# Sums in the order of x, zero borders written in the prologue, the residual inside silu's products, and the last strips' statistics taken one by one

## The chip, the cores and the metric

The kernel runs on one core of a Trainium2 chip. The metric is the device time of one execution, in microseconds (us). The core has five engines that take instructions in their own order and wait for each other by semaphores: TensorE (PE, matrix products), VectorE (DVE), ScalarE (ACT), GpSimd (POOL) and SyncE (SP, which here only issues DMAs). POOL and ACT can issue DMAs too. The fast memory has 128 partitions; a tile written "128x512" has 512 floats in each.

## The reference

Two layers on x of shape 4 x 16 x 256 x 256 (batch, channel, row, column), everything in fp32. `_gn` is a group norm with 8 groups of 2 channels.

```python
def _L0_conv_ref(x, conv_w, conv_b):
    out = jax.lax.conv_general_dilated(x, conv_w, window_strides=(1, 1), padding='SAME', ...) + conv_b[None, :, None, None]
    logits = out.reshape(N, C, K * K, H, W)          # C = 16, K = 5: 400 logits a pixel
    weights = jax.nn.softmax(logits, axis=2)
    return jnp.einsum('ncuij,ncuij->ncij', _unfold(x), weights)   # 5x5 patches, weighted

def _L1_conv_ref(x, base_weight, spline_weight, spline_scaler, bias_weight):
    patches = _extract_patches(x, KSIZE, STRIDE, PAD)             # 3x3
    bspl = _b_splines(patches, grid)                              # 8 cubic bases of each value
    out = jnp.einsum('bjhwn,ijn->bihw', jax.nn.silu(patches), base_w)
    out = out + jnp.einsum('bjhwns,ijns->bihw', bspl, spl_w)
    return out + bias_weight[None, :, None, None]

x = x + _L0_conv_ref(_gn(x), L0_conv_conv_w, L0_conv_conv_b)
x = x + _L1_conv_ref(_gn(x), L1_conv_base_weight, ...)
```

So layer 0 makes, for every pixel and channel, 25 logits by a 3x3 convolution, and averages the 5x5 patch by their softmax. Layer 1 is a convolution of silu(x) and of eight spline bases of x.

## The kernel before

**Prologue.** It loads x, takes batch statistics, prepares the weights, and normalizes batch 0 into three scratch areas in DRAM: `hs` (patches), `hst` and `hsl` (the convolution's operands, high and low parts). `normalize(b, ...)` is a generator: each `next` does one piece. Its first piece writes the zero borders of these areas by twelve DMAs (lines 256, 262 and 263); for batch 0 they go on POOL's queue, for the batches 1 to 3 on SP's. Batch b+1 is normalized while layer 0 works on batch b, one piece per step; its x loads are line 276, the tile is `xp`, and ACT's normalizing lines are 323 and 336. `prepare0` and `prepare1` prepare the weights of the two layers; a part of both runs on POOL.

**Layer 0.** There are 64 strips (4 batches, 2 halves of 128 rows, 8 strips of 32 columns), with the row in the partition. A strip has 8 steps of 4 columns. A step does, each on its own engine:

- PE: the logits `lg` (lines 791 and 795), into PSUM
- ACT: their exponentials into `e[:, 0]` (line 814)
- POOL: `e[:, 1] = e[:, 0] * u`, the product with the patches (line 819)
- DVE: one reduction over the 25 taps of both halves of `e`, into `nd` (line 691). This is done two steps late.

After a strip's last reduction, with delays counted in steps (`after(k, f)` puts f k steps later): ACT takes the reciprocal of the denominator as Ln and Exp (`seed`, lines 704 and 705), DVE refines it and multiplies (`divide`, lines 709, 710 and 713), POOL subtracts the result from x in place (`apply`, line 719; the sign is turned in line 710). `nd` holds columns then channels, x holds channels then columns, so line 713 writes `o` transposed:

```python
o = ndp.tile([P, C, SW], F32, name=f"o_{n}{arm}", tag="o", bufs=2)
nc.vector.tensor_mul(o.rearrange("p c j -> p j c"), nd[:, 1], r)
```

The x tile `xc` holds four strips (CX = 128 columns). When its last strip is subtracted, `statistics` runs once for each of 8 groups on ACT (line 731: Identity, then Square, each with an accumulated sum; the written values go to the scratch tile `z` and are not used), and `store` writes the tile to `x1s` in DRAM (line 740, ACT's queue). `e` has four buffers, `nd` and `xc` three each, `z` two in the pool `l0`.

**Layer 1.** There are 64 units of 16 rows. The splines need, for a row of the unit, the distance of each value to the bases' centres: SP loads replicated rows into `xta`, `xtb`, `xtc` in turn, ACT takes the absolute distance (line 942) and squares (lines 164, 166 and 167), DVE does the rest (lines 159, 168, 169 and 170), in two halves of the unit with the temporaries `ta` and `tb`; line 170 writes `ring`, from which PE reads. `silu` (ACT, line 924) reads the tile `sx` (64 partitions: 4 rows of 16 channels) and writes `sl`. The output `yp` of a unit is 128 products: 96 of `ring` with `wt` (line 988), 8 of `sx` with an identity `wx`, which is the residual x (line 996), and 24 of `sl` with `ws` (line 1004). DVE adds the bias into `yo` (line 971) and SP stores it.

**Order.** `in_order` fixes every engine's instructions in the order in which they were written. Layer 1's first instructions may start ahead of layer 0's end on two engines only, behind marks that layer 0 leaves (`marks[SPE]`, `marks[ACTE]`); the first silu comes behind layer 0's last ACT instruction. Layer 1's tiles take the memory of layer 0's pools when these are free.

Of the kernel before, what the change touches and what calls it, by code (L numbers as in the profile page):

```python
# [11 lines left out]
F32 = mybir.dt.float32  # L12
# [4 lines left out]
PSUM = bass.MemoryType.PSUM  # L17
DRAM = bass.MemoryType.DRAM


# [13 lines left out]
def conv_preact_kernel(  # L34
# [84 lines left out]
    nc.gpsimd.memset(wt, 0.0)  # L119
    ws = const.tile([RD * C, 3, RT, C], F32, name="ws")  # L120
    nc.gpsimd.memset(ws, 0.0)

    wx = const.tile([RD * C, RT, C], F32, name="wx")
    nc.gpsimd.memset(wx, 0.0)
    for r in range(RT):
        p = SROWS.index(r + 1) * C
        nc.sync.dma_start(wx[p : p + C, r], ident[p : p + C, p : p + C])

# [4 lines left out]
    NK = NH * W // CX  # L133
    st1 = [const.tile([P, 2, G, NK], F32, name=f"st1_{b}") for b in range(B)]

# [111 lines left out]

    def normalize(b, ptr, tiles, held=None, copier=None, queue=nc.sync):

# [3 lines left out]
        copier = copier or nc.scalar.copy  # L253
        for e in (0, HP - PAD):
            for r in range(PAD):
                queue.dma_start(
                    hs[b][:, e + r].rearrange("s c w -> c s w"),
                    zero[0:C, 0 : NST * SP].rearrange("c (s w) -> c s w", s=NST),
                )
        for h in range(NH):  # L260
            for w in (0, (W + 1) * RP):
                queue.dma_start(hst[b][h][:, w : w + RP], zero[0:C, 0:RP])
                queue.dma_start(
                    hsl[b][h][:, :, w : w + RP].rearrange("c t r -> (c t) r"), zero[:, 0:RP]
                )

        moves = []
# [132 lines left out]
    with tc.tile_pool(name="prep0", bufs=2) as prep, tc.tile_pool(  # L400
# [121 lines left out]
        for b in range(B):  # L522
# [38 lines left out]
            nc.vector.tensor_scalar(v, v, 9.0 / 8.0, ms[:, 0:1], ALU.mult, ALU.add)  # L561
            nc.vector.tensor_scalar(v, v, ms[:, 1:2], None, ALU.mult)
            if b == 0:
                prepare0()
            if b == 1:
                prepare1()
            if b == 0:
                ahead = normalize(0, ptr0, tiles, held, nc.vector.tensor_copy, nc.gpsimd)
                next(ahead)
# [41 lines left out]
    def layer0(shift):  # L611
# [4 lines left out]
        with tc.tile_pool(name=f"prep{arm}", bufs=2) as prep, tc.tile_pool(  # L616
# [62 lines left out]
            def after(k, f, *args):  # L679

                later.append([k, partial(f, *args)])
# [7 lines left out]
            def sums():  # L689
                nd, j, e, done = waiting.pop(0)  # L690
                nc.vector.tensor_reduce(  # L691
                    nd[:, :, j : j + JG, :], e.rearrange("p t j m c d -> p t j c m d"),
                    AX.XY, ALU.add,
                )
                if done is not None:
                    done()
# [5 lines left out]
            def seed(n, nd, xc):  # L702
                r = prc.tile([P, SW, C], F32, name=f"r_{n}{arm}", tag="r")
                nc.scalar.activation(r, nd[:, 0], AF.Ln)
                nc.scalar.activation(r, r, AF.Exp, scale=-1.0)
                after(1, divide, n, nd, xc, r)

            def divide(n, nd, xc, r):
                nc.vector.tensor_mul(nd[:, 0], nd[:, 0], r)
                nc.vector.scalar_tensor_tensor(r, nd[:, 0], 2.0, r, ALU.subtract, ALU.mult)  # L710

                o = ndp.tile([P, C, SW], F32, name=f"o_{n}{arm}", tag="o", bufs=2)
                nc.vector.tensor_mul(o.rearrange("p c j -> p j c"), nd[:, 1], r)  # L713
                after(LAG + 3, apply, n, o, xc)

            def apply(n, o, xc):
                w0 = strips[n][2] * SW % CX
                v = xc[:, :, w0 : w0 + SW]
                nc.gpsimd.tensor_sub(v, v, o)  # L719
                if w0 + SW == CX:  # L720
                    for g in range(G):
                        after(1 + g, statistics, n, xc, g)
                    after(2, store, n, xc)

            def statistics(n, xc, g):
                b, hf, s = strips[n]
                k = hf * (W // CX) + s * SW // CX
                z = l0.tile([P, GC * CX], F32, name=f"z_{n}_{g}{arm}", tag="z")
                v = xc[:, g * GC : (g + 1) * GC, :].rearrange("p c w -> p (c w)")
                for t, f in enumerate((AF.Identity, AF.Square)):  # L730
                    nc.scalar.activation(  # L731
                        z, v, f, scale=nrm[b][:, 0, g : g + 1], bias=nrm[b][:, 1, g : g + 1],
                        accum_out=st1[b][:, t, g, k : k + 1],
                    )
# [21 lines left out]
            for n, (b, hf, s) in enumerate(strips):  # L756
# [14 lines left out]

                nd = ndp.tile([P, 2, SW, C], F32, name=f"nd_{n}{arm}", tag="nd")
                for j in range(0, SW, JG):
# [68 lines left out]
    def layer1(arm, last, marks):  # L842
# [3 lines left out]
        with ExitStack() as pools:  # L846
# [14 lines left out]
            xt0, tmp0 = fixed("xta", XT), temps("ta")  # L861
            sxp, yop = pool("sx", 2), pool("yo", 3)
            tmp1, xt1 = temps("tb"), fixed("xtb", XT)
            ring = fixed("ring", [P, 3 * RU + 2, W + 2])[0]
            sl, xtt = fixed("sl", [RD * C, RU // RT, W + 2], 2), xt0 + xt1 + fixed("xtc", XT)
            pad = fixed("pad", [P, W + 2])[0]
# [32 lines left out]


            def load_tiles(n):
                b, u = units[n]
                t = sxp.tile([RD * C, RU // RT, W], F32, name=f"sx_{n}{arm}", tag="sx")
                for p, q in outside(u):
                    nc.gpsimd.memset(t[p : p + C, q], 0.0)  # L905
                for k, d in enumerate(SROWS):
                    q0 = 1 if (u, d) == (0, 0) else 0
                    q1 = RU // RT - (1 if (u, d) == (NU - 1, RD - 1) else 0)
                    nc.sync.dma_start(
                        t[k * C : (k + 1) * C, q0:q1, :],  # L910
                        rows(x1s[b], [[CP, C], [RT * W, q1 - q0], [1, W]], u * RU - 1 + d + q0 * RT),
                    )
                return t

# [6 lines left out]

            def silu(n, t):
                b, u = units[n]
                nc.scalar.activation(  # L924
                    sl[n % 2][:, :, 1 : W + 1], t, AF.Silu,
                    scale=sc[b][0][0 : RD * C], bias=sc[b][1][0 : RD * C],
                )
                for p, q in outside(u):
                    nc.gpsimd.memset(sl[n % 2][p : p + C, q, 1 : W + 1], 0.0)

# [50 lines left out]

            def outputs(n, sx):
                b, u = units[n]
                yp = py.tile([P, 2, W], F32, name=f"yp_{n}{arm}", tag="yp")
                M, r0 = RT * C, place(n)
                for k, (d, e) in enumerate((d, e) for d in range(RD) for e in range(3)):
                    for t in range(NT):
                        nc.tensor.matmul(  # L988
                            yp[t * M : (t + 1) * M],
                            lhsT=wt[:, d, e].rearrange("p r o -> p (r o)"),  # L990
                            rhs=ring[:, r0 + t * RT + d : r0 + t * RT + d + 9 : 8, e : e + W],
                            start=k == 0, stop=False,
                        )

                for t in range(NT):
                    nc.tensor.matmul(  # L996
                        yp[t * M : (t + 1) * M],
                        lhsT=wx.rearrange("p r o -> p (r o)"),
                        rhs=sx[:, t : t + NT + 1 : NT],
                        start=False, stop=False,  # L1000
                    )
                for e in range(3):
                    for t in range(NT):
                        nc.tensor.matmul(  # L1004
                            yp[t * M : (t + 1) * M],
                            lhsT=ws[:, e].rearrange("p r o -> p (r o)"),
                            rhs=sl[n % 2][:, t : t + NT + 1 : NT, e : e + W],
                            start=False, stop=e == 2,
                        )
                waiting.append((b, u, yp))  # L1010
# [5 lines left out]
            for half in range(2):  # L1016
                load_x(0, half)
            sx = [load_tiles(0)]
            for half in range(2):
# [11 lines left out]
            first_silu = len(nc.cur_bb.bb.instructions)  # L1031
            silu(0, sx[0])
            for n in range(len(units)):
                if n % 2:
                    next(more, None)
                if n > 0:
                    features(n, put)
                    silu(n, sx[n])
                halo(n)
# [4 lines left out]
                if n + 1 < len(units):  # L1044
                    sx.append(load_tiles(n + 1))
                outputs(n, sx[n])
            for _ in range(LAG1):
# [59 lines left out]
```

## Time and profile before

| | us |
|---|---|
| median of three runs | 3093.68 (3092.81 to 3095.0) |
| the profiled execution | 3092.67 |
| its span, first to last instruction | 3090.9 |
| prologue, to the first strip | 0 to 119 |
| layer 0 | 119 to 2073 |
| layer 1 | 2073 to 3091 |

The largest groups, with their mean durations in ns:

| instruction | engine | how many | mean |
|---|---|---|---|
| reduction, line 691 | DVE | 512 | 3476 |
| products of `divide`, lines 709, 710, 713 | DVE | 64 each | 681, 696, 1083 |
| product with the patches, line 819 | POOL | 512 | 3547 |
| subtraction, line 719 | POOL | 64 | 1328 |
| exponentials, line 814 | ACT | 1024 | 837 |
| one pass of the statistics, line 731, and the read of its sum | ACT | 256 each | 600 and 192 |
| residual product, line 996 | PE | 512 | 601 |

How it is read: "busy" is the time in which an engine runs an instruction, and a bracket behind an instruction, such as `[11.10 <-POOL e L819]`, says how long its engine stood idle before it and which instruction ended that. Instructions of one engine overlap a little at their ends, so what one of them costs is read from start to start.

### The profile page before, as it was taken

Reading aid. Unit: us, or ns where it says so; the run is one execution under the profiler, and the core shown is the slowest. Engines: PE = TensorE matmul, PEld = TensorE weight load, DVE = VectorE, ACT = ScalarE, POOL = GpSimd, SP = SyncE. Lnnn points to the kernel's source line nnn. Section 1 sums busy time; section 2 is a strip of 40 time slices with the busy share of each in tenths; the row PEclk is TensorE's granted clock in tenths of the full one; section 3 lists DMA queues with packets and bytes.
Section 4 is the critical chain, followed back from the end, with each engine's and each line's share of the span. In section 5 each row is a group of like instructions: output and inputs, shape, how many; then the busy total and the mean of one; then the engine's idle time right before and its main releaser. Section 6 shows DMA issues by size and latency. Waiting matters only on the chain.

```text
span 3090.9 us, 40797 instructions
## 1 busy us (share of the span) xinstructions
PE 2840.5 (92%) x14760; PEld 1484.6 (48%) x14760; DVE 2976.4 (96%) x1571; ACT 2240.5 (72%) x2619; POOL 1951.1 (63%) x734
## 2 busy tenths in 40 slices
PE   4499999989999999999999999957999999999998
PEld 3366656656556666666666566632222222222222
DVE  7499999999999999999999999988999999999997
ACT  6466665676766566756646546559999999999995
POOL 4199999999999999999999999970100100000000
PEclk7699999999999999999999999988999999999999
DMA  9988977879878778878867667649999988999994
GB/s 275 284 222 224 249 203 206 219 189 255 230 206 240 191 202 224 242 214 218 221 161 199 164 171 193 156 110 201 194 193 197 197 194 191 197 196 198 193 198 89
DMA packets 352725, 626.36 MB, mean 203 GB/s; under 512 B 41330, under 2 KB 218724, under 8 KB 336644
## 3 DMA queue, kind: packets, MB, share of 16 engines
q1 hardware_dynamic: 318020, 605.29, 79.0%
q10 hardware_dynamic: 33024, 16.78, 1.9%
q8 instruction: 121, 1.98, 0.3%
q0 software_dynamic: 1472, 1.59, 0.2%
q14 instruction: 88, 0.72, 0.1%
HBM read 513.95 MB, written 104.24 MB: 200 GB/s over the span
## 4 chain that ended last, share of the span: by engine, by line
DVE 65%; PE 9%; ACT 9%; issue 8%; DMA 6%; SPq 2%; POOL 1%; DVEq 0%; ACTq 0%; POOLq 0%
DVE nd L691 45%; PE yp L988 3%; PE lg L791 3%; DVE ta L169 3%; DVE ta L168 3%; DVE tb L169 3%; DVE tb L168 3%; DMA sx<-x1s 2%; DVE ring L170 2%; DVE o L713 1%; DVE tb L159 1%; DVE r L710 1%; DMA an<-hsl 1%; ACT sl L924 1%; ACT ta L167 1%
## 5 line engine op out<-in xcount | busy, mean ns | idle before, releaser
L791 PE MATMUL lg<-wm,am 128*128 128x400 f32 x4096 | 1741.2, 506 | 102.9 <-ACT e L814 64.2
L819 POOL TENSOR_TENSOR e<-e,u 128x1600 f32<-128x1600 f32 x512 | 1789.9, 3547 | 67.7 <-ACT e L814 48.6
L691 DVE TENSOR_REDUCE nd<-e 128x128 f32<-128x3200 f32 x512 | 1746.9, 3476 | 31.6 <-POOL e L819 31.5
L795 PE MATMUL lg<-wn,an 97*128 97x400 f32 x2048 | 1349.7, 659 | 12.1 <-DMA an<-hsl 11.9
L814 ACT ACTIVATE e<-lg 128x800 f32<-128x800 f32 x1024 | 817.8, 837 | 726.4 <-DVE nd L691 522.3
L791 PEld LDWEIGHTS lg<-wm,am 128*128 128x128 f32 x4096 | 764.3, 193 | 424.1 <-ACT e L814 113.3
L988 PE MATMUL yp<-ring,wt 128*32 128x512 f32 x6144 | 739.7, 595 | 66.8 <-POOL ring L959 46.5
L795 PEld LDWEIGHTS lg<-wn,an 97*128 97x128 f32 x2048 | 389.3, 190 | 330.3 <-issue 21.1
L988 PEld LDWEIGHTS yp<-ring,wt 128*32 128x32 f32 x6144 | 206.9, 109 | 591.5 <-issue 470.0
L905 POOL MEMSET sx<- 16x256 f32 x8 | 2.4, 302 | 667.2 <-PE yp L996 232.5
L1004 PE MATMUL yp<-sl,ws 64*32 64x512 f32 x1536 | 176.5, 588 | 0.0
L731 ACT ACTIVATE z<-xc,nrm 128x256 f32<-128x256 f32 x256 | 153.6, 600 | 10.5 <-POOL xc L719 6.2
L170 DVE SCALAR_TENSOR_TENSOR ring<-ta,ta 128x2048 f32<-128x2048 f32 (+1 forms) x64 | 147.8, 2309 | 10.8 <-ACT z L731 8.3
L169 DVE TENSOR_TENSOR ta<-ta,ta 128x2048 f32<-128x2048 f32 (+1 forms) x64 | 148.4, 2318 | 2.9 <-ACT ta L167 2.9
L170 DVE SCALAR_TENSOR_TENSOR ring<-tb,tb 128x2048 f32<-128x2048 f32 x64 | 145.6, 2276 | 2.6
L169 DVE TENSOR_TENSOR tb<-tb,tb 128x2048 f32<-128x2048 f32 x64 | 145.2, 2268 | 0.7 <-ACT tb L167 0.7
L924 ACT ACTIVATE sl<-sx,q 64x2048 f32<-64x2048 f32 x64 | 133.4, 2085 | 1.5 <-DMA sx<-x1s 1.4
L194 POOL TENSOR_TENSOR d<-d,nrz 128x8 f32<-128x8 f32 x4 | 2.7, 663 | 200.1 <-DVE d L192 200.1
L167 ACT ACTIVATE ta<-ta 128x2048 f32<-128x2048 f32 (+1 forms) x64 | 123.2, 1925 | 2.0
L167 ACT ACTIVATE tb<-tb 128x2048 f32<-128x2048 f32 x64 | 120.5, 1883 | 0.0
L1004 PEld LDWEIGHTS yp<-sl,ws 64*32 64x32 f32 x1536 | 48.8, 106 | 116.2 <-issue 115.9
L719 POOL TENSOR_TENSOR xc<-xc,o 128x512 f32<-128x512 f32 x64 | 85.0, 1328 | 13.4 <-DVE o L713 13.4
(181 smaller groups left out, 2054.3 us busy)
## 6 DMA issues: line engine op xcount, KB each, us to landing
am<-hst SPq DMA_DIRECT2D x512, 194.6 KB
u<-hs SPq DMA_DIRECT2D x320, 288.0 KB
an<-hsl SPq DMA_DIRECT2D x512, 129.8 KB
xta<-x1s SPq DMA_DIRECT2D x40, 1024.0 KB
xtb<-x1s SPq DMA_DIRECT2D x40, 1024.0 KB
xtc<-x1s SPq DMA_DIRECT2D x40, 1024.0 KB
am<-hst SPq DMA_DIRECT2D x256, 129.8 KB
sx<-x1s SPq DMA_DIRECT2D x248, 128.0 KB
```

The lines of the kernel that those rows point to most:

```text
L167: nc.scalar.activation(s1, r1, AF.Square, scale=2.0)
L168: nc.vector.scalar_tensor_tensor(s2, t, 2.0, s2, ALU.subtract, ALU.mult)
L169: nc.vector.tensor_mul(s1, s1, r1)
L170: nc.vector.scalar_tensor_tensor(f, s2, 0.0, s1, ALU.min, ALU.subtract if given else ALU.add)
L691: nc.vector.tensor_reduce(nd[:, :, j : j + JG, :], e.rearrange("p t j m c d -> p t j c m d"), AX.XY, ALU.add,)
L791: nc.tensor.matmul(lg[:, i, :NL], lhsT=am[:, o : o + P], rhs=wm.rearrange("p m c d -> p (m c d)"), start=True, stop=False,)
L795: nc.tensor.matmul(lg[:, i, :NL], lhsT=an[:, o : o + P], rhs=wn.rearrange("p m c d -> p (m c d)"), start=False, stop=True,)
L814: nc.scalar.activation(ev, lg[:, :, :NL], AF.Exp)
L819: nc.gpsimd.tensor_tensor(e[:, 1].rearrange("p j m c d -> p j (m c) d"), e[:, 0].rearrange("p j m c d -> p j (m c) d"), uv, ALU.mult,)
L924: nc.scalar.activation(sl[n % 2][:, :, 1 : W + 1], t, AF.Silu, scale=sc[b][0][0 : RD * C], bias=sc[b][1][0 : RD * C],)
L988: nc.tensor.matmul(yp[t * M : (t + 1) * M], lhsT=wt[:, d, e].rearrange("p r o -> p (r o)"), rhs=ring[:, r0 + t * RT + d : r0 + t * RT + d ...
L1004: nc.tensor.matmul(yp[t * M : (t + 1) * M], lhsT=ws[:, e].rearrange("p r o -> p (r o)"), rhs=sl[n % 2][:, t : t + NT + 1 : NT, e : e + W], ...
```

## The change

Five edits go together.

1. *Zero borders.* A function `zeros(b)` issues the twelve DMAs of batch b on POOL's queue, and the prologue calls it for every batch, right after the batch's statistics. `normalize` no longer does so.
2. *Sums in the order of x.* `nd` is laid out as channels then columns. The reduction writes it in that order, its reads are unchanged; line 713 becomes an in-place product on `nd[:, 1]`; the tile `o` is gone, and the subtraction reads `nd[:, 1]`.
3. *Statistics of the last columns.* For the last four strips, `statistics` is called after each strip's subtraction on its 32 columns instead of once for 128; the table of sums of the last batch has three more columns.
4. *Scratch.* `z` moves from the pool `l0` (two buffers) to the pool `x1` of the x tiles (one buffer).
5. *Residual in silu's products.* SP loads the rows straight into partitions 64 to 127 of `sl`, which now has three buffers; silu reads these and writes partitions 0 to 63. The identity moves into the lower rows of the centre tap of `ws`, so that the eight centre products take 128 rows instead of 64, and the eight products with `wx` are gone: 120 products a unit. The tiles `sx` and `wx` are gone.

```diff
-    def normalize(b, ptr, tiles, held=None, copier=None, queue=nc.sync):
+    def zeros(b):
         for e in (0, HP - PAD):
             for r in range(PAD):
-                queue.dma_start(
+                nc.gpsimd.dma_start(
                     hs[b][:, e + r].rearrange("s c w -> c s w"),
...
+            zeros(b)
             if b == 0:
                 prepare0()
             if b == 1:
                 prepare1()
...
                 nc.vector.tensor_reduce(
-                    nd[:, :, j : j + JG, :], e.rearrange("p t j m c d -> p t j c m d"),
+                    nd[:, :, :, j : j + JG].rearrange("p t c j -> p t j c"),
+                    e.rearrange("p t j m c d -> p t j c m d"),
                     AX.XY, ALU.add,
                 )
...
                 nc.vector.scalar_tensor_tensor(r, nd[:, 0], 2.0, r, ALU.subtract, ALU.mult)
-
-                o = ndp.tile([P, C, SW], F32, name=f"o_{n}{arm}", tag="o", bufs=2)
-                nc.vector.tensor_mul(o.rearrange("p c j -> p j c"), nd[:, 1], r)
-                after(LAG + 3, apply, n, o, xc)
+                nc.vector.tensor_mul(nd[:, 1], nd[:, 1], r)
+                after(LAG + 3, apply, n, nd, xc)
...
-                nc.gpsimd.tensor_sub(v, v, o)
+                nc.gpsimd.tensor_sub(v, v, nd[:, 1])
+                few = n >= len(strips) - CX // SW
+                if few or w0 + SW == CX:
+                    for g in range(G):
+                        after(1 + g, statistics, n, xc, g, w0 if few else 0, w0 + SW)
                 if w0 + SW == CX:
-                    for g in range(G):
-                        after(1 + g, statistics, n, xc, g)
                     after(2, store, n, xc)
...
-                z = l0.tile([P, GC * CX], F32, name=f"z_{n}_{g}{arm}", tag="z")
+                z = x1p.tile([P, GC, CX], F32, name=f"z_{n}_{g}{arm}", tag="z", bufs=1)
...
-                nd = ndp.tile([P, 2, SW, C], F32, name=f"nd_{n}{arm}", tag="nd")
+                nd = ndp.tile([P, 2, C, SW], F32, name=f"nd_{n}{arm}", tag="nd")
...
-                t = sxp.tile([RD * C, RU // RT, W], F32, name=f"sx_{n}{arm}", tag="sx")
+                t = sl[n % 3][P // 2 :, :, 1 : W + 1]
...
+                t = sl[n % 3][0 : P // 2, :, 1 : W + 1]
                 nc.scalar.activation(
-                    sl[n % 2][:, :, 1 : W + 1], t, AF.Silu,
-                    scale=sc[b][0][0 : RD * C], bias=sc[b][1][0 : RD * C],
+                    t, sl[n % 3][P // 2 :, :, 1 : W + 1], AF.Silu,
+                    scale=sc[b][0][P // 2 :], bias=sc[b][1][P // 2 :],
                 )
...
-                for t in range(NT):
-                    nc.tensor.matmul(
-                        yp[t * M : (t + 1) * M],
-                        lhsT=wx.rearrange("p r o -> p (r o)"),
-                        rhs=sx[:, t : t + NT + 1 : NT],
-                        start=False, stop=False,
-                    )
                 for e in range(3):
                     for t in range(NT):
+                        v = slice(0, P if e == 1 else P // 2)
                         nc.tensor.matmul(
                             yp[t * M : (t + 1) * M],
-                            lhsT=ws[:, e].rearrange("p r o -> p (r o)"),
-                            rhs=sl[n % 2][:, t : t + NT + 1 : NT, e : e + W],
+                            lhsT=ws[v, e].rearrange("p r o -> p (r o)"),
+                            rhs=sl[n % 3][v, t : t + NT + 1 : NT, e : e + W],
                             start=False, stop=e == 2,
                         )
```

## The prediction

> **What bounds the kernel now.** I read the page's busy shares first, then the chain of waits, then each stage by a table of windows, then one strip's timeline. The page and the chain point to VectorE (DVE):
>
> ```profile
> PE 2840.5 (92%) x14760; PEld 1484.6 (48%) x14760; DVE 2976.4 (96%) x1571; ACT 2240.5 (72%) x2619; POOL 1951.1 (63%) x734
> DVE 65%; PE 9%; ACT 9%; issue 8%; DMA 6%; SPq 2%; POOL 1%; DVEq 0%; ACTq 0%; POOLq 0%
> ```
>
> Shares over the whole span mix two stages, so here are windows inside each of them: the first is two strips of layer 0, the second nearly all of layer 1. Columns: window, its length, busy time per engine.
>
> ```profile
> 1878.00:1937.00 59.00, 57.06 (x193) 36.45 (x192) 58.86 (x23) 32.85 (x52) 59.00 (x19) 0.97 0.77 196
> 2130.00:3046.00 916.00, 900.68 (x7680) 247.32 (x7675) 911.14 (x500) 902.68 (x424) 31.93 (x28) 1.00 0.92 194
> ```
>
> DVE is full in both: 58.86 of 59.0 and 911.1 of 916. In layer 0 GpSimd (POOL) is full beside it; in layer 1 PE and ACT stand 10 us behind. So a DVE instruction taken off a strip is worth its time, until POOL ends last; PE work taken off a unit of layer 1 is worth nothing while DVE keeps its pace. One strip on DVE:
>
> ```profile
> 1878.03 0.70 DVE L709 TENSOR_TENSOR nd<-nd,r 128x512 f32<-128x512 f32 x1
> 1878.77 0.70 DVE L710 SCALAR_TENSOR_TENSOR r<-nd,r 128x512 f32<-128x512 f32 x1
> 1879.49 1.11 DVE L713 TENSOR_TENSOR o<-nd,r 128x512 f32<-128x512 f32 x1
> 1880.43 27.22 DVE L691 TENSOR_REDUCE nd<-e 128x128 f32<-128x3200 f32 x8
> 1907.56 0.68 DVE L709 TENSOR_TENSOR nd<-nd,r 128x512 f32<-128x512 f32 x1
> ```
>
> Start to start it is 29.53. Two products of the same size, L709 and L713, cost 0.70 and 1.11; they differ in that L713 writes o transposed, each float 128 bytes from the one before.
>
> **B. Sums and product in order of x.** The eight reductions stay, with the same reads in the same order; only their output addresses change, from 16 adjacent floats to steps of 128 bytes. L713 becomes an in-place contiguous product like L709. Today the reduction starts 0.94 after L713 does (1880.43−1879.49). An ordinary 0.68 product ahead of a reduction (lo L366, 186.23 to 186.83) releases it after 0.60. Gain 0.34 a strip; by mean durations (L713 1083 ns, L709 681) it would be 0.40. For 63 strips that another follows: 21.4 (or 25). POOL must keep up: eight products L819, 3.48 apart, plus 1.23 for the subtraction are 29.1 a strip, and DVE's new period is 29.49−0.34=29.15. So POOL just lets it happen. Where POOL ends last some 4 of the 21 are lost: low end 18.
>
> What does the reductions' new output cost? No row shows a strided reduction. The nearest row is L713: (1083−681)/512 = 0.785 ns for each float written at that stride. The Trainium skill ("SBUF — State Buffer", section "Door 1: The DMA port swizzle", note on cachelines) says the memory has lines of 16 bytes and that an access crossing into a new one pays a penalty, which agrees with that row and speaks against this change: 128 writes × 0.785 = 0.10 a reduction, ×512 = 51 us lost. Against it: a reduction writes one float for 25 reads, 3476/128 = 27 ns apart, and L713 one per 1.3 ns, so the write has time to hide. I take 0 (bounds 0 and +51; below zero nothing, the reads are the same). By the rule the sum would be some 22 slower than before.
>
> POOL's subtraction now reads nd in the order of x as it read o: same price. nd is held until then, about a strip longer; it has 3 buffers, where two would be live.
>
> **A. Zero borders.** Today batch 1's zeros stand on SP's queue ahead of its first x loads, at the start of layer 0:
>
> ```profile
> 135.87 3.18 SPq L256 DMA_DIRECT2D hs<-zero  x4
> 143.16 0.42 SPq L263 DMA_DIRECT2D hsl<-zero  x1
> 143.62 0.98 SPq L276 DMA_DIRECT2D xp<-in_x_dram  x2
> ...
> 147.91 0.87 ACT L323 ACTIVATE hsp<-xp,nrm 128x576 f32<-128x576 f32 x1 [12.32 <-DMA xp<-in_x_dram]
> ...
> 153.85 3.49 DVE L691 TENSOR_REDUCE nd<-e 128x128 f32<-128x3200 f32 x1 [11.10 <-POOL e L819]
> ```
>
> ACT waits 12.32 for xp with the exponentials queued behind it; PE, POOL and DVE starve. Without the zeros xp is issued at about 135.9, 7.7 earlier. The DMA engines are busy to about 140 (share 1.04 in 135–140, 0.17 in 140–145), so xp lands about 142 rather than 147.7: −5.7 (−3 to −8, the whole shift). Batches 2 and 3 start inside full DVE work, where SP has slack: nothing.
>
> The price is in the prologue: 36 more DMAs on POOL's queue, at 0.50–0.54 each (its L256/L262/L263 rows) 18 us. They stand ahead of the weights' preparation (wm, wp, the 2.95-us product L494) and of batch 2's and 3's rstd; batch 1's rstd falls between them. POOL is 31% busy to 119 (36.74), and the bound there is DMA, share 0.96, with slack at 40–60. What follows on ACT and DVE (whi, wn) has until 119, the first strip. I take +0.5 (−3 to +3); if the weights came last, each microsecond would count in full.
>
> **C, D. z and the last strips' statistics.** z moves to the pool of x1's tiles, so ring, xtc and pad now sit on memory that must wait for the last z, while xtb and the tb temporaries do not. The boundary today:
>
> ```profile
> 2076.78 0.60 ACT L731 ACTIVATE z<-xc,nrm 128x256 f32<-128x256 f32 x1 [6.04 <-POOL xc L719]
> 2087.39 1.91 ACT L164 ACTIVATE tb<-xta 128x2048 f32<-128x2048 f32 x1
> 2087.45 2.56 DVE L170 SCALAR_TENSOR_TENSOR ring<-ta,ta 128x2304 f32<-128x2304 f32 x1 [8.29 <-ACT z L731]
> 2099.55 3.81 ACT L942 ACTIVATE xtb<-xtb,q 128x4096 f32<-128x4096 f32 x1 [3.09 <-DMA xtb<-x1s]
> 2137.46 1.22 DVE L159 TENSOR_SCALAR tb<-xta 128x2048 f32<-128x2048 f32 x1
> ```
>
> Of the last four strips, each now has its own 8 groups: 32 groups, not 8, two passes of 64 elements each. A group of 256 takes 1.32 today; less 192 elements at L166's 0.92 ns twice, 0.96; I take 1.1. Those of strips 60 and 61 fit where ACT is half idle. Sixteen are left at the end: 16×1.1 = 17.6 against 10.6, but 12 of these passes, and layer 1's first squares (tb), now stand in ACT's order ahead of strip 63's r, while it waited 7.85 + 6.04. Working this through: last products about 2076.5 (today 2073), z ends about 2093–2095 (2087.4), so ring's first write moves from 2087.45 to about 2095. Behind that write DVE holds the rest of unit 0. But ACT's squares are done by then, xtb (issued today at 2087.39 only after z) is loaded, and unit 1's first distance comes at about 2098.5 instead of 2099.55. After it units run at their pace of 15.26 without the 3.09, 1.45 and 1.37 stalls: unit 3, today 2137.46, at about 2135. Gain 2.3 (7 gained to 6 lost: z's own 7-us delay with nothing won back).
>
> **E. Residual in silu's products.** Eight matmuls of 128 a unit go; the rows L996 read now stand in the upper half of sl and pass with the centre taps, K=128 for 64. Per unit PE drops 0.88 (2897.53 to 2898.41). But DVE's spacing sets it: yo L971 from 2894.82 to 2910.08 is 15.26, and PE waited on ring:
>
> ```profile
> 2902.35 9.22 PE L988 MATMUL yp<-ring,wt 128*32 128x512 f32 x84 [0.20 <-DVE ring L170]
> 3080.55 2.76 PE L1004 MATMUL yp<-sl,ws 64*32 64x512 f32 x24
> ```
>
> So 0 in the steady stage, hidden by DVE; after the last ring write (3069.18) only PE remains, and it ends 0.9 earlier, less 0.2 that it will have waited: −0.7. silu itself changes halves of the partitions, same shape, 2.1 each on an ACT that has slack.
>
> **Sum.** −21.4 −5.7 +0.5 −2.3 −0.7 = −29.6. The profiled execution took 3092.67 (span 3090.9 and 1.8 around it), 1.0 below the median 3093.68. So 3063.1 for that execution, 3064 against the median.
>
> **Rivals.** (1) The stride costs in the reductions: +51 −29.6 gives 3115, slower. It decides from 29.6/512 = 0.058 a reduction, 58% of L713's price. For: L713's row; against: 27 ns between writes. 7%. A partial price near that point: within the bound, 3%. (2) POOL becomes layer 0's bound, or the boundary loses: half of B and a later ring, 3071 to 3080. For: 29.09 against 29.15, and z's later end; 18%. (3) PE's relief counts: 64×0.88 = 56 less the 0.7 already in the sum gives 3009; against it DVE's 911 of 916. Or B gives 0.40 and the start 8: 3057. The first 2%, other gains below 3055 4%. (4) The change does not do what it says: every edit is in each engine's order of instructions, so no weight.
>
> **Numbers.** Likeliest case, 66%: 3064, 3055 to 3071. With (2) up to 3077, about 10% are left above (mostly rival 1) and 6% below. A difference of 0.2% (6.2 us) is about what this kernel's measurement can tell. Faster 0.90, same 0.03, slower 0.07.
>
> **What would show it.** Right: reductions still 3.476; the in-place product 0.68; a strip 29.15 start to start; POOL with hardly an idle 0.05 a strip; ACT's wait for xp at 142; layer 1 units 15.26 with PE's wait for ring grown to about 1; last z about 2094 less the 27 gained before it. Wrong: reductions over 3.53; POOL spacing 29.4; the first reduction after 135.8; units shorter than 15.2.

## The result and the profile after

The changed kernel takes 3070.18 us (median of four runs, 3068.97 to 3073.02) against 3093.24 for the kernel before on the same chip (four runs). The ratio is 0.9926, with a 95% interval of 0.9909 to 0.9943. It is 23 us faster, where 29.6 had been worked out; the forecast of 3064 is 6 too low, the range of 3055 to 3077 holds it. The profiled execution took 3069.49, with a span of 3067.7.

The busy shares of the page, and then the windows in the two stages:

```profile
PE 2790.4 (91%) x14248; PEld 1444.1 (47%) x14248; DVE 2954.1 (96%) x1571; ACT 2268.3 (74%) x2715; POOL 1965.1 (64%) x771
```

```profile
1878.00:1937.00 59.00, 56.39 (x197) 36.30 (x196) 58.86 (x23) 27.28 (x37) 59.00 (x19) 1.00 0.67 181
2130.00:3020.00 890.00, 843.26 (x6991) 213.63 (x6994) 885.27 (x486) 883.25 (x411) 26.15 (x29) 1.00 0.95 195
```

DVE is as full as before: 58.86 of 59.0 in layer 0, 885.3 of 890 in layer 1. PE in layer 1 has fallen to 843 of 890, and nothing came of it. One strip on DVE in the timeline, and then, from the view of the tile nd, the two rows that the prediction turned on (count, then minimum, median and maximum in ns, then the first and last start):

```profile
1860.22 0.68 DVE L716 TENSOR_TENSOR nd<-nd,r 128x512 f32<-128x512 f32 x1
1860.93 0.70 DVE L717 SCALAR_TENSOR_TENSOR r<-nd,r 128x512 f32<-128x512 f32 x1
1861.66 0.69 DVE L718 TENSOR_TENSOR nd<-nd,r 128x512 f32<-128x512 f32 x1
1862.26 27.23 DVE L697 TENSOR_REDUCE nd<-e 128x128 f32<-128x3200 f32 x8
1889.41 0.68 DVE L716 TENSOR_TENSOR nd<-nd,r 128x512 f32<-128x512 f32 x1
```

```profile
L697 DVE TENSOR_REDUCE nd<-e x512: 3474/3478/3490, 138.9 to 2044.2; 128x128 f32<-128x3200 f32 x171
L718 DVE TENSOR_TENSOR nd<-nd,r x64: 686/686/687, 194.1 to 2058.3; 128x512 f32<-128x512 f32 x64
```

The product that wrote o transposed took 1082 in the median; in place it takes 686. The reductions took 3476 and now take 3478, although every float that they write is 128 bytes from the last. A strip is 29.19 from start to start. Of the strips with nothing else in between, that is the median of twenty; before, the median of twenty was 29.49 (the strip that the prediction shows, 29.53, is the longest of them). The gain of a strip is 0.30.

Where the 23.2 us of the two spans come from, by the times at which stages end in the two traces ("the first lo" is the first piece of batch 1's normalizing on DVE, the row L366 before):

| stretch | predicted | measured | measured from |
|---|---|---|---|
| prologue and start of layer 0, to the first lo on DVE | −5.2 | −1.0 | 186.23 to 185.24 |
| from there to the end of the last reduction | −21.4 | −18.9 | 1881.4 to 1862.5 |
| from there to the start of unit 3 on DVE | −2.3 | −2.4 | 69.85 to 67.43 |
| from there to the end | −0.7 | −0.9 | 953.4 to 952.6 |

So the boundary and the tail came out as worked out. The start lost most of its gain, and the strips gave a little less. Each row compares one execution with one other: over all the traces of the experiments below, the second stretch is 1881.4 to 1884.0 without edit 2 and 1862.1 to 1865.0 with it, so a difference of 2 in that row means little. The start, in the timeline of SP, ACT and DVE:

```profile
123.28 1.88 SPq L645 DMA_DIRECT2D am<-hst  x3
139.86 0.97 SPq L281 DMA_DIRECT2D xp<-in_x_dram  x2
146.95 0.87 ACT L328 ACTIVATE hsp<-xp,nrm 128x576 f32<-128x576 f32 x1 [8.24 <-DMA xp<-in_x_dram]
152.90 3.49 DVE L697 TENSOR_REDUCE nd<-e 128x128 f32<-128x3200 f32 x1 [7.01 <-POOL e L826]
```

xp is issued at 139.86 and not at 135.9, because layer 0's first loads (am) now go out at 123.28; they went out at 119.11 before. The prologue is 4.2 longer. The boundary, DVE and ACT:

```profile
2055.59 0.58 ACT L711 ACTIVATE r<-nd 128x512 f32<-128x512 f32 x1
2056.82 0.69 DVE L716 TENSOR_TENSOR nd<-nd,r 128x512 f32<-128x512 f32 x1 [9.12 <-ACT r L712]
2074.90 2.56 DVE L173 SCALAR_TENSOR_TENSOR ring<-ta,ta 128x2304 f32<-128x2304 f32 x1 [9.94 <-ACT z L737]
2078.24 3.80 ACT L951 ACTIVATE xtb<-xtb,q 128x4096 f32<-128x4096 f32 x1
2115.12 1.22 DVE L162 TENSOR_SCALAR tb<-xta 128x2048 f32<-128x2048 f32 x1
```

The last reduction ends at 2047.69. Ring's first write comes 27.2 after it, 19.8 before the change. The first distance of unit 1 comes 30.5 after it against 31.9, and no longer waits for xtb. In layer 1 PE waits for the ring in every unit, 0.79 in the median where it was 0.20. After the last ring write the last products take 13.5 where they took 14.1, which DVE's wait for them shows. PE's rows after, then DVE's last row before and after:

```profile
2895.48 10.52 PE L997 MATMUL yp<-ring,wt 128*32 128x512 f32 x94 [0.79 <-DVE ring L173]
2905.93 3.05 PE L1007 MATMUL yp<-sl,ws 64*32 64x512 f32 x24
```

```profile
3083.38 0.75 DVE L971 TENSOR_SCALAR yo<-yp,bias_sb 128x512 f32<-128x512 f32 x1 [13.54 <-PE yp L1004]
3060.66 0.75 DVE L980 TENSOR_SCALAR yo<-yp,bias_sb 128x512 f32<-128x512 f32 x1 [12.95 <-PE yp L1007]
```

### The profile page after: what moved, and what is told of

It is laid out like the page before. It is cut to its first block, busy times and chain, and to the rows that moved or that the text cites. A ratio compares the mean times of both kernels' runs of the same rounds, so it can differ in the third digit from the quotient of the medians.

```text
span 3067.7 us, 39878 instructions
## 1 busy us (share of the span) xinstructions
PE 2790.4 (91%) x14248; PEld 1444.1 (47%) x14248; DVE 2954.1 (96%) x1571; ACT 2268.3 (74%) x2715; POOL 1965.1 (64%) x771
## 4 chain that ended last, share of the span: by engine, by line
DVE 63%; PE 13%; issue 10%; DMA 6%; ACT 4%; SPq 2%; POOL 1%; DVEq 0%; ACTq 0%; POOLq 0%
DVE nd L697 39%; PE lg L798 10%; DVE ta L172 4%; DVE ta L171 4%; DVE tb L172 4%; DVE tb L171 4%; PE lg L802 3%; DVE tb L162 2%; DVE yo L980 1%; DMA an<-hsl 1%; DVE r L717 1%; DMA xin<-in_x_dram 1%; DMA am<-hst 1%; DMA sl<-x1s 1%; DVE nd L716 1%
## 5 line engine op out<-in xcount | busy, mean ns | idle before, releaser
L697 DVE TENSOR_REDUCE nd<-e 128x128 f32<-128x3200 f32 x512 | 1748.0, 3478 | 27.0 <-POOL e L826 26.8
L1007 PE MATMUL yp<-sl,ws 64*32 64x512 f32 (+1 forms) x1536 | 195.3, 602 | 0.0
L737 ACT ACTIVATE z<-xc,nrm 128x256 f32<-128x256 f32 (+1 forms) x304 | 172.4, 567 | 6.7 <-POOL xc L724 1.1
L933 ACT ACTIVATE sl<-sl,q 64x2048 f32<-64x2048 f32 x64 | 134.0, 2094 | 1.8 <-DMA sl<-x1s 0.2
L1007 PEld LDWEIGHTS yp<-sl,ws 64*32 64x32 f32 (+1 forms) x1536 | 29.9, 106 | 161.0 <-issue 154.3
L724 POOL TENSOR_TENSOR xc<-xc,nd 128x512 f32<-128x512 f32 x64 | 84.5, 1321 | 17.0 <-DVE nd L718 17.0
```

The source lines that it names most:

```text
L697: nc.vector.tensor_reduce(nd[:, :, :, j : j + JG].rearrange("p t c j -> p t j c"), e.rearrange("p t j m c d -> p t j c m d"), AX.XY, ALU.add,)
L737: nc.scalar.activation(z[:, :, w0:w1], xc[:, g * GC : (g + 1) * GC, w0:w1], f, scale=nrm[b][:, 0, g : g + 1], bias=nrm[b][:, 1, g : g + 1] ...
L1007: nc.tensor.matmul(yp[t * M : (t + 1) * M], lhsT=ws[v, e].rearrange("p r o -> p (r o)"), rhs=sl[n % 3][v, t : t + NT + 1 : NT, e : e + W], ...
```

## The experiments

Each ratio is to the kernel before, on the same chip as the run. Executions of one kernel lie 1 to 14 us apart, and of the variants of the changed kernel only one, the normalizing later, has an interval clear of that of the change. What tells the variants apart is therefore read from the stages in the traces, as in the table above, one execution each.

**The sums alone.** Before, with `nd` as `[P, 2, C, SW]` and the product in place.

```diff
-                o = ndp.tile([P, C, SW], F32, ...)
-                nc.vector.tensor_mul(o.rearrange("p c j -> p j c"), nd[:, 1], r)
+                nc.vector.tensor_mul(nd[:, 1], nd[:, 1], r)
```

> The kernel before with edit 2 alone (reductions in the order of x, in-place product). Theory: the gain of layer 0 is this edit and nothing else, 0.30 a strip from start to start (29.49 to 29.19), 63 strips, 18.9 us; reductions stay 3.393 apart; everything outside layer 0's steady strips moves as a block. Time 3093.2-18.9 = about 3074. Rival (the gain of a strip needs the other edits, or POOL ends last without them): under 15 us, 3078 or more, with DVE waiting for POOL in the steady strips. If the strided output cost anything in the reductions they would stand further apart than 3.393.

Measured: 3076.22, ratio 0.994 (0.9923 to 0.9956), 17.7 less than before. In the trace a strip is 0.30 shorter, in the median of the differences, strip by strip, of the two traces:

```profile
1864.63 0.68 DVE L710 TENSOR_TENSOR nd<-nd,r 128x512 f32<-128x512 f32 x1
1866.08 0.69 DVE L712 TENSOR_TENSOR nd<-nd,r 128x512 f32<-128x512 f32 x1
1866.68 27.23 DVE L691 TENSOR_REDUCE nd<-e 128x128 f32<-128x3200 f32 x8
1893.83 0.68 DVE L710 TENSOR_TENSOR nd<-nd,r 128x512 f32<-128x512 f32 x1
```

29.20 from start to start, reductions 3.393 apart as before. DVE waited for POOL 2.7 in all between 186 and 2040 (2.1 before and after). So this edit makes layer 0's gain by itself. The span of the profiled execution is 16.1 shorter (3074.8 against 3090.9): its start is 2.8 longer, with xp issued at 145.68 and not at 143.62, and what follows the first lo is 18.9 shorter.

**The zeros alone.** Before, with `zeros(b)` on POOL's queue in the prologue.

> The kernel before with edit 1 alone (all zero borders on POOL's queue in the prologue). Theory: the first loads of layer 0 are issued some 4 us later than before since the added DMAs take the DMA engines' time while they are full, and xp, no longer behind the zeros on SP, lands only about 1 us earlier; first lo of layer 0 on DVE (186.2 before) at about 185.2, the total 3092, within the noise of no change. Rival (the delay of the prologue came from the other edits): first loads of layer 0 at 119, first lo near 181, the total 3088.

Measured: 3091.52, ratio 0.9993 (0.9986 to 1.0): hardly to be told from no change. The delay of the prologue is there with this edit alone: first loads at 123.80, xp issued at 140.35, first lo at 185.21 (before: 119.11, 143.62, 186.23).

**Only batch 1's zeros.** After, with those of batches 2 and 3 back on SP.

```diff
-            zeros(b)
+            if b < 2:
+                zeros(b, nc.gpsimd)
...
+        if b > 1:
+            zeros(b, nc.sync)
```

> The kernel after with only batch 1's zeros in the prologue (behind batch 0's, on POOL's queue); those of batches 2 and 3 back on SP at the start of the batch before, as in the kernel before. Theory (DMA time): batch 1's zeros run at 38 to 46 where the DMA engines had slack, and what delayed the prologue by 4.2 were the zeros of batches 2 and 3 at 51 to 68, where hs, hst, hsl and xin go out. First loads of layer 0 at 119 to 120.5 (after: 123.3), xp issued about 136 to 137, first lo on DVE 2 to 4 earlier than in after, 3066 to 3068. Rival (POOL's order): batch 1's zeros are the ones that push the preparation of the weights (wm, the 2.95 product, wp) back on POOL; if that is what the prologue pays, first loads stay at 123 and the time at 3070.

Measured: 3068.79, ratio 0.9915 (0.9899 to 0.9932). The time is just above what was expected. First loads at 120.90, xp issued at 137.21, first lo at 180.92, 4.3 before that of after. The preparation of the weights on POOL is as late as in after, to 0.02, while the first loads are 2.4 earlier, so these 2.4 are not paid there. In the other 1.8 the rival is at work. The rows of before, of after and of this kernel, first on POOL, then on ACT, then the first store of hs in this stretch and the load of the next xin on SP:

```profile
44.42 1.03 POOL L472 COPY wp<-wnr 97x80 f32<-97x80 f32 x5
54.77 0.51 ACT L476 CAST wn<-wp 32x400 fp32r<-32x400 f32 x1
58.43 0.36 SPq L284 DMA_DIRECT2D hs<-hsp  x1
64.13 0.89 SPq L419 DMA_DIRECT2D xin<-in_x_dram  x1
```

```profile
49.89 1.04 POOL L477 COPY wp<-wnr 97x80 f32<-97x80 f32 x5
56.06 0.52 ACT L481 CAST wn<-wp 32x400 fp32r<-32x400 f32 x1 [1.47 <-DVE wn L480]
58.97 0.36 SPq L289 DMA_DIRECT2D hs<-hsp  x1
67.23 0.84 SPq L424 DMA_DIRECT2D xin<-in_x_dram  x1
```

```profile
49.88 1.03 POOL L479 COPY wp<-wnr 97x80 f32<-97x80 f32 x5
56.59 0.52 ACT L483 CAST wn<-wp 32x400 fp32r<-32x400 f32 x1 [2.21 <-DVE wn L482]
59.50 0.36 SPq L291 DMA_DIRECT2D hs<-hsp  x1
65.21 0.88 SPq L426 DMA_DIRECT2D xin<-in_x_dram  x1
```

With batch 1's zeros on POOL, wp is ready 5.5 later, DVE makes wn at 55.99 instead of 51.32, and ACT, which has the next normalizing pieces behind its own part of wn, stands waiting for DVE's. The stores of hs go out 1.1 later than in the kernel before, and so does the next xin. All five traces with these zeros in the prologue have that wait, 1.1 to 2.2 long; none of the other seven has it.

With the zeros of batches 2 and 3 the stretch from that store to the next xin is longer: 8.26 in after, 7.9 to 8.3 in the four traces that have these zeros, 5.7 in the eight that have not. So the 4.2 of after are 0.5 up to the store, 2.6 from there to the next xin, and 1.1 from there to the first loads; the 1.8 of this kernel are 1.1, 0.0 and 0.7. The last part was not followed up. It varies by 0.8 among the seven traces without added zeros.

What fits the 2.6 is the DMA engines' time. The view of the DMA queues from 20 to 125, before and then after (packets, MB, share of the 16 engines), and the same five microseconds of both, whose last two columns are the DMA share and GB/s:

```profile
q0 software_dynamic: 896, 0.97, 3.5%
60.00:65.00 5.00, 0.44 (x3) 0.15 (x1) 5.00 (x13) 5.00 (x4) 0.00 (x0) 0.50 1.05 364
```

```profile
q0 software_dynamic: 2043, 1.49, 6.4%
60.00:65.00 5.00, 0.00 (x0) 0.00 (x0) 5.00 (x14) 5.00 (x5) 5.00 (x11) 0.50 0.97 258
```

The added zeros are 2.9% of 105 us, 3.0 us of all sixteen engines, for half a megabyte in small packets. With batch 1's zeros alone the share is 4.2%, so those of batches 2 and 3 take 2.2% or 2.3 us, about what the stretch has grown by. At 60 to 65 the engines are about as full as before and move 258 GB/s in place of 364. There hs, hst and hsl go out, and the load of the next xin stands behind them in SP's queue.

**Zeros behind the loads.** After, with batch 0's zeros alone in the prologue. Those of the other batches go on SP behind the batch's first x loads, one every second step:

```diff
         for h in range(NH):
             load(0, h)
+        if held is None:
+            moves.extend((12 + 2 * i, f) for i, f in enumerate(zeros(b, nc.sync)))
         yield
```

> The kernel after with the zeros of batches 1 to 3 on SP again, but behind the batch's first x loads, one every second step. Theory: the prologue is the one of before (first loads of layer 0 at 119), xp is issued at about 136 instead of 139.9 and lands at about 142, as the prediction had it; first lo on DVE 4 earlier than in after, 3066. Rival (the landing is bound by the DMA engines and not by the issue): xp still lands at 146 and the first lo stays within 1.5 of after, 3069.

Measured: 3066.02, ratio 0.9909 (0.9892 to 0.9925), 4.2 better than after by the medians; the first lo comes 4.8 earlier than in after.

```profile
118.77 1.87 SPq L649 DMA_DIRECT2D am<-hst  x3
135.87 0.97 SPq L282 DMA_DIRECT2D xp<-in_x_dram  x2
142.63 0.87 ACT L329 ACTIVATE hsp<-xp,nrm 128x576 f32<-128x576 f32 x1 [8.60 <-DMA xp<-in_x_dram]
```

Issued at 135.87, landed at 142.6, first lo at 180.45, 5.8 before that of the kernel before. This is the −5.7 that the prediction had for the start, without the price in the prologue.

**Statistics whole.** After, without the split of the last strips:

```diff
-                few = n >= len(strips) - CX // SW
+                few = False
```

> The kernel after without edit 3: statistics of all 64 strips once for 128 columns, z still in the pool of the x tiles. Theory: edit 3 is a loss inside a boundary that edit 4 made better. 32 passes of 64 elements follow the last subtractions at 0.567 each where 16 of 256 at 0.66 would do, and they also hold back r of the last strip by 6 us. Without it r follows the last reduction, z ends some 19 us after the last reduction instead of 27, ring's first write comes 7.5 earlier, and the first distance of unit 1 4 to 6 earlier: 3063 to 3066, i.e. 4 to 7 below the kernel after. Rival (edit 3 is what brings the boundary's 2.4 us, the tb squares going ahead of the last z): slower than the kernel after, 3072 to 3078.

Measured: 3066.80, ratio 0.9914 (0.9897 to 0.9931), just above what was expected. The last reduction ends at 2049.94; r follows at once, ring 22.2 after it (27.2 in after), the first distance of unit 1 25.6 after it (30.5), unit 3 62.4 after it (67.4).

```profile
2049.97 0.60 ACT L711 ACTIVATE r<-nd 128x512 f32<-128x512 f32 x1 [7.56 <-DVE nd L697]
2053.10 0.69 DVE L716 TENSOR_TENSOR nd<-nd,r 128x512 f32<-128x512 f32 x1 [3.16 <-ACT r L712]
2072.17 2.56 DVE L173 SCALAR_TENSOR_TENSOR ring<-ta,ta 128x2304 f32<-128x2304 f32 x1 [10.94 <-ACT z L737]
2075.51 3.80 ACT L951 ACTIVATE xtb<-xtb,q 128x4096 f32<-128x4096 f32 x1
2112.32 1.22 DVE L162 TENSOR_SCALAR tb<-xta 128x2048 f32<-128x2048 f32 x1
```

So edit 3 costs 5.0 inside a boundary whose sum is a gain. In after, ACT is busy without a gap from 2047.78 to silu's table load at 2074.83: 5.7 of squares, r, and 37 passes of the statistics. The last pass releases ring's first write in both kernels. A pass of 64 elements with the read of its sum takes 0.567 from start to start, one of 256 takes 0.66 in the mean in the kernel before and 0.72 here: a quarter of the elements saves at most 0.16. So 37 small passes are about 21 us of ACT and 16 large ones about 11.5. Of the 9.5 between them 4.2 come back, because a distance (2.1) and a wait for the last subtraction (2.2) no longer stand ahead of the last pass.

**z back in its pool.** The last kernel with z in `l0` again, so without edits 3 and 4.

> The kernel after without edits 3 and 4: statistics of all strips once for 128 columns, z back in the pool l0 with two buffers. Theory: the boundary is that of the kernel before with edit 5 (unit 3 starts 68.6 after the last reduction; 62.4 with z among the x tiles in e4_whole, 67.4 in after), because xtb's load waits for the last z again; total about 3070 to 3073, so edit 4 alone is worth 6 and edit 3 took 5 of them back. Rival (z's place makes no difference, only the number of passes): unit 3 at 62 to 63 as in e4_whole, 3066.

Measured: 3072.04, ratio 0.9925 (0.9908 to 0.9941). xtb's load is issued at 2067.02, with the end of z, and unit 3 starts 69.6 after the last reduction.

```profile
2067.02 1.16 SPq L903 DMA_DIRECT2D xtb<-x1s  x2
2079.52 3.81 ACT L951 ACTIVATE xtb<-xtb,q 128x4096 f32<-128x4096 f32 x1 [3.44 <-DMA xtb<-x1s]
```

With z among the x tiles (the run before this one) the first distance of unit 1 has no such wait. Edit 4 is thus worth 7.2 at the boundary, edit 3 took 5.0 of them back.

**The residual alone.** Before, with edit 5.

> The kernel before with edit 5 alone (residual in the centre products, rows loaded into the upper half of sl, three buffers). Theory: units of layer 1 keep 15.26 because DVE sets them; the tail after the last ring write is about 0.7 shorter; with three buffers the rows of unit 1 can be loaded a little earlier than sx's, so 0 to 1.5 more at the boundary: 3091 to 3093. Rival (PE's relief of 0.88 a unit counts): 56 us less, 3037.

Measured: 3091.92, ratio 0.9992 (0.9983 to 1.0001): no difference that can be told. Units stay 15.25 apart in the median, as before, and PE is busy 858 of 905 in layer 1, DVE 900:

```profile
2135.00:3040.00 905.00, 858.18 (x7123) 215.79 (x7117) 900.18 (x493) 898.13 (x418) 25.67 (x29) 1.00 0.96 196
```

**Both mended.** Edits 2, 4 and 5, with the zeros behind the loads.

> Edits 2, 4 and 5, no edit 3, zeros spread on SP behind the first x loads. Theory: the two gains add, 4 at the start and 5 at the boundary: 3061 to 3063. Rival (the earlier start is lost in layer 0's waits for loads): as e4_whole, 3066.

Measured: 3063.31, ratio 0.9908 (0.9886 to 0.9931). The boundary is that of the statistics taken whole (unit 3 starts 62.8 after the last reduction). xp lands at 144.2 in this execution, with 10.5 of wait on ACT.

**Normalizing later.** The same, with four empty steps behind the loads of a batch:

```diff
             moves.extend((12 + 2 * i, f) for i, f in enumerate(zeros(b, nc.sync)))
+            for _ in range(4):
+                yield
```

> e8_spread_whole with four empty steps between the first x loads of a batch and the first normalizing instruction, so that ACT reaches the instruction that waits for xp only after xp has landed. Theory: what the start of layer 0 still pays is ACT standing on that wait (10.5 in e8, 8.6 in e6) with the exponentials behind it; with four steps between (about 3.4 each, 14 in all) the wait is gone, DVE has its third reduction at 143 to 145 instead of 149 to 150, and 4 to 8 go: 3055 to 3059. Rival (the start is bound by the DMA engines, which are still filling the strip's own loads): PE or POOL waits for am, an or u in its place, and the time stays within 2 of e8.

Measured: 3059.29, ratio 0.9887 (0.987 to 0.9903). This is the fastest of the kernels measured here, 36 below the kernel before and by its ratio 0.4% below the change as it was made. ACT's wait is gone; DVE now runs four reductions in a row from 134.07, and what is left there are waits of about 1:

```profile
134.07 13.94 DVE L703 TENSOR_REDUCE nd<-e 128x128 f32<-128x3200 f32 x4 [17.19 <-POOL e L832]
149.31 6.97 DVE L703 TENSOR_REDUCE nd<-e 128x128 f32<-128x3200 f32 x2 [1.30 <-POOL e L832]
157.24 24.43 DVE L703 TENSOR_REDUCE nd<-e 128x128 f32<-128x3200 f32 x7 [0.96 <-POOL e L832]
```

The third reduction starts at about 141.0, earlier than I expected; the time is 0.3 above what I expected. By the second strip's products DVE is 7.6 ahead of the kernel without the empty steps (212.1 against 219.7), and at the last reduction 4.2: layer 0 gives 3.3 back on the way. 2.1 of these are DVE's waits for POOL in that stretch, 5.2 in all against 3.1; why they grew was not followed up.

**Statistics in halves.** The same with the last four strips' statistics in two halves.

> e9_late with the statistics of the last four strips in two halves of 64 columns (strips 60 and 61, then 62 and 63). Theory: the passes behind the last subtraction stay 16 but are 0.06 to 0.1 shorter each (128 elements in place of 256; 64 elements took 0.567 with the read of the sum, 256 took 0.72 from start to start), so z ends 1 to 2 earlier and the first distance of unit 1 too: 1 to 2 below e9. Rival (the earlier 16 passes delay r of the last strip as the four quarters did): unit 3 over 64 after the last reduction, slower than e9 by 1 to 3.

Measured: 3063.52, ratio 0.9898 (0.9882 to 0.9915). The rival was right:

```profile
2052.83 0.69 DVE L722 TENSOR_TENSOR nd<-nd,r 128x512 f32<-128x512 f32 x1 [9.39 <-ACT r L718]
```

The passes of strips 60 and 61 are handed out one group a step, between layer 1's first squares. The last of them, and the squares, still stand ahead of r. Unit 3 starts 65.5 after the last reduction (62.4 in the run before). That is 3.1 of the 6.4 by which the spans of the two profiled executions differ; 2.3 lie ahead of the last reduction and 1.0 after unit 3, and were not followed up. The intervals of the two ratios overlap, so the 3.1 at the boundary is what this run shows.

## Why the prediction was right or wrong

**Right: what bounds the stages.** DVE sets both, and the strip's gain came from the one instruction it was put down to. The strided output of the reductions costs 2 ns of 3476. The row of L713 did not carry over (0.785 ns a float would have made 100), and the reason given, 27 ns between two writes, is in accord with that; no run varied the number of reads. The penalty for crossing into a new line that the Trainium skill states ("SBUF — State Buffer", section "Door 1: The DMA port swizzle") agrees with the row of the transposed product; in the reductions it is 2 ns at most, and the measurement decides. Rival (1) is out.

**Mis-sized: 0.34 a strip.** The term took one strip's start-to-start time from L713 to the next reduction, 0.94. Over the 51 strips where a reduction follows directly it is 0.923 in the mean, and the in-place product's is 0.605. That makes 0.32. Eight reductions, 1 to 2 ns longer each, and a few ns elsewhere make it 0.30: 18.9 over 63 strips, within the bound of 18 given. It was not POOL: DVE's waits for POOL in layer 0's steady part are 2.1 before and after, so rival (2)'s first half is out too.

**Failed: the price in the prologue.** "I take +0.5 (−3 to +3)" was 4.2, outside its own range. Two steps of it failed. The first is the slack at 40 to 60. I counted POOL's issue time and left the engines' time out of the sum. The average there, 0.65, hides 0.98 at 45 to 50 and 0.88 at 50 to 55. The emptiest stretch, 55 to 60, can't be used: POOL works in order, its rstd there waits for DVE, and the zeros behind it are issued from 57.8 on, when the engines fill again. The stores and the next xin fell 2.6 behind there. The second is "What follows on ACT and DVE (whi, wn) has until 119": ACT works in order too, and the pieces behind wn feed the stores at 58. That was 0.5 here and 1.1 with batch 1's zeros alone. The last 1.1 of the 4.2 stay open. With none of the added zeros the price is gone, and then the −5.7 comes as worked out (5.8).

**Right, by parts that were not told apart: the boundary.** Ring's first write was forecast 7.5 later against the last reduction and came 7.4 later; the first distance 1.05 earlier and came 1.4 earlier; the whole −2.3 and is −2.4. The runs show it as +5.0 of edit 3 and −7.2 of edit 4. The prediction saw that the passes delay r and ring, and did not price what the boundary would be without them. It had the last products 3.5 later, and they came 5.6 later; that cost nothing by itself, because ring waits for the last z and not for them.

**Right: PE's relief.** The wait for ring has grown by 0.6 a unit, units keep 15.25, and only the tail became shorter: the products behind the last ring write by 0.6, where 0.9 less 0.2 was worked out. The rest of the tail's 0.9 is behind the last products and is not PE's.

## What to carry to other kernels

Moving DMAs out of the way of a queue was only free where the DMA engines had room: look at their share and GB/s in the window where they will land, and at what the issuing engine waits for there, before counting the slack. Look also at who waits for the issuing engine's next instructions: an engine that works in order passes such a delay on to everything behind it. A wait that an in-order engine takes for a load can be removed by a few steps between the load and its first use; here that was worth 7.6 at the start and 4.2 at the end of the layer. Cutting an epilogue into smaller pieces pays only if the pieces run before the end: a pass over a quarter of the elements took more than three quarters of the time, so the same work in four times the passes kept the engine longer ahead of what waited for it.

## What the runs showed of the hardware

A reduction of 25 floats to one on VectorE writes at a stride of 128 bytes for the same price as side by side (3478 and 3476 ns), while a product of 512 floats pays 0.40 us for that stride (1082 and 686 ns). ScalarE's pass with an accumulated sum takes 0.44 us for 64 elements and 0.60 for 256, plus 0.19 for the read of the sum. Half a megabyte of zeros in packets of some 450 bytes (0.52 MB in 1147 packets) cost the sixteen DMA engines 3.0 us, about 170 GB/s, where they move over 300 in the same stage.
